# Two self-attention layers in fp32: hand-ordered queues, two more split steps, and projections moved between layers

## The chip, the cores and the metric

The kernel runs on one core of a Trainium2 chip. Five engines work side by side, each with its own queue of instructions: TensorE (PE, matrix products; PEld is its weight load), VectorE (DVE), ScalarE (ACT), GpSimd (POOL, which here only issues DMAs) and SyncE (SP, which issues DMAs as well). The metric is the time of one execution on the device in microseconds (us); the kernel before takes 3156.2 us, the median of three runs (3154.14 to 3157.11).

## The reference

The input x is 4 images of 64x64 = 4096 tokens with 256 channels. Each layer is attention of all tokens of an image with each other. Layer 0 has queries and keys of 32 channels and values of 256, and a residual with a factor gamma; layer 1 has values of 128 channels and an output matrix to 256.

```python
# layer 0
q = x @ Wq + bq; k = x @ Wk + bk; v = x @ Wv + bv
attn = softmax(q k^T)
x = gamma * (attn @ v) + x
# layer 1
f = x @ Wf + bf; g = x @ Wg + bg; v = x @ Wh + bh
beta = softmax(g f^T)
out = x + (beta @ v) @ Wo + bo
```

All of it is fp32. The matrix of 4096x4096 scores of each image and layer is never stored; it is made and used up tile by tile.

## The kernel before, in words

**fp32 from cheaper products.** [...] So the kernel can split a factor p into `high`, `low` and a difference `d`, the values likewise into three forms, and add three fp32r products (a *split* step), or it takes one true fp32 product (a *whole* step). Splitting costs a second exponential on ACT (L542, `high`) beside the first (L544, `p`), and two passes on DVE (L555 `low`, L560 `d`). In layer 0 every step is split. In layer 1 the steps named in SPLIT1 are, 6 of 16.

**Steps and blocks.** Work is a list of steps, in the order image b, layer l, query block j, step i. In layer 0 a block has 256 queries and eight steps of 512 keys; there are 16 blocks, 128 steps an image. In layer 1 a block has 512 queries and 16 steps of 256 keys; there are 8 blocks, again 128 steps. Each step has an exponential of 128x1024 elements. Iteration n of the main loop (L738) issues the `d` of step n (`cut_both`), the `low` of step n+1 (`cut_low`), the sum of p (`add_up`, layer 1 only, L573), the scores and exponentials of step n+2 (`later.scores`, L532), units of other work, and the products of step n (L582 in layer 0, L600 in layer 1).

**Sums.** In layer 0 the sum of the exponentials comes out of the products (two more columns in the values). In layer 1 DVE adds p into `p_sum` (L571, L573); for the five steps in MOVED_SUMS a DMA that accumulates does it (L548, L550, issued by POOL), and its result is added at the block's end (L662), followed by the fold of two halves (L663).

**Projections.** Tokens go in halves of 256, 16 an image. For each half and layer there are three units: `transpose_unit` (eight DMAs load 32x32 squares, L280; DVE transposes, L392; ACT and DVE cut the result into `xh` and `xl`, L405, L406), `qk_unit` (four matmuls L422, then ACT and DVE in turn, L439 to L442, and a store to `qk_dram`, from where POOL loads keys and queries, L493), and `v_unit` (matmuls L464 and the cut of the values, L480 to L487). Layer 1's halves need the result of layer 0's blocks, which goes through `x1_dram` (L636).

**Where they stand.** `plan` puts units into iterations. In layer 0, block j projects half j-2 for layer 1; the last two halves come in layer 1's first block. The next image's halves, queries, keys and values alike, are projected in layer 1, one every seven steps. `ends` finish a block in the next one's first iterations: residuals in layer 0 (L629 to L643), outputs in layer 1 (L670 to L678).

**What sets the order.** The program is traced in this order, but the framework's planner then orders each engine's instructions anew, by priority and by its own estimate of when they are ready, before the kernel is built. On the chip each engine's queue is fixed.

**Buffers.** The 128x1024 tiles live in named rings: two of `t`, three of `p`, two of `l`, one of `d` and one of `e`, nine in all (L267). The squares, `xh` and `xl` share a ring of two. PSUM holds the accumulators, `st` for scores, `pair` (accumulators in layer 0, a second scores buffer in layer 1) and two side buffers.

Of the kernel before, what the change touches and what calls it, by code (L numbers as in the profile page):

```python
# [65 lines left out]
AHEAD = 3  # L66

SPLIT1 = (0, 3, 5, 8, 11, 13)
MOVED_SUMS = (0, 4, 7, 9, 12)
# [169 lines left out]
def fast_path(ctx: ExitStack, tc: tile.TileContext, x, w0, w1, wo, bo, gamma, out, off):  # L239
# [15 lines left out]
    V1 = NI[1] - sum(split[1])  # L255

# [8 lines left out]


    def wide(tag, name, dtype=F32):  # L267
        return work.tile([P, 2 * QB], dtype, tag=tag, bufs={"d": 1, "e": 1, "p": 3}.get(tag, 2), name=name)

# [36 lines left out]
    ident = const.tile([P, P], F32, name="ident")  # L306
# [12 lines left out]
    bv = const.tile([P, C], F32, name="bv0")  # L319
# [3 lines left out]
    bo_sb = const.tile([P, C], F32, name="bo")  # L323
    for l, (q_w, q_b, k_w, k_b, v_w, v_b) in enumerate((w0, w1)):
        queue = (nc.scalar, nc.gpsimd)[l]
        w_sb = work.tile([P, NCC, 2 * D], F32, tag="small", bufs=4, name=f"wqk_whole{l}")
        b_sb = const.tile([2 * D, 1], F32, name=f"bqk{l}")
        for g, w_dram, b_dram in ((0, q_w, q_b), (D, k_w, k_b)):
            queue.dma_start(w_sb[:, :, g : g + D], w_dram.rearrange("(c p) d -> p c d", p=P))
            queue.dma_start(b_sb[g : g + D, :], b_dram.rearrange("(d o) -> d o", o=1))  # L330
# [9 lines left out]
    nc.gpsimd.dma_start(bv, w0[5].partition_broadcast(P))  # L340
    nc.gpsimd.dma_start(bv1, w1[5].rearrange("(c o) -> c o", o=1))
    nc.gpsimd.dma_start(wo_sb, wo)
    nc.gpsimd.dma_start(bo_sb, bo.partition_broadcast(P))
# [16 lines left out]
    def bias_units():  # L360


        def issue():
            nc.vector.tensor_scalar(bv, bv, gamma_sb, None, ALU.mult)
            wide_bias = work.tile([P, P], F32, tag="small", bufs=4, name="wide_bias")
            nc.vector.memset(wide_bias, 1.0)
            nc.vector.tensor_scalar(wide_bias, wide_bias, bv1, None, ALU.mult)
            ps = side_psum("ps_bias")[:, :C]
            nc.tensor.matmul(ps, wide_bias, wo_sb, start=True, stop=True)
            nc.vector.tensor_add(bo_sb, bo_sb, ps)  # L370

        return [issue]

    xT, x_parts, k_t, v_t, halves = {}, {}, {}, {}, {}
    qk_dram, x1_dram = {}, {}
    q_t, moved_sums, first_p, waiting = {}, {}, [], {}


    def transpose_unit(b, l, h):
        def issue():  # L380
            key = (b, l, h)
            lead = b == l == 0 and h % 2 == 1
# [8 lines left out]
            else:  # L391
                nc.vector.transpose(  # L392
                    xT[key].rearrange("p c n -> p (c n)"), turned[key].rearrange("p c n -> p (c n)")
                )
            x_parts[key] = [
# [9 lines left out]
            nc.scalar.copy(x_parts[key][0], xT[key])  # L405
            nc.vector.tensor_sub(x_parts[key][1], xT[key], x_parts[key][0].bitcast(F32))  # L406
# [3 lines left out]
        return issue  # L410

    def project_units(b, l, h):

        key = (b, l, h)
        j, part = divmod(h, 2)
        cols = slice(part * QB0, (part + 1) * QB0)

        def qk_unit():
            ps = side_psum(f"psqk_{b}_{l}_{h}")[:, :QB0]
            for c in range(NCC):  # L420
                for n in range(2):
                    nc.tensor.matmul(  # L422
                        ps,
                        wqk[l][:, c, :],
                        x_parts[key][n][:, c, :],
                        start=(c == n == 0),
                        stop=(c == NCC - 1 and n == 1),
                    )
            whole = data.tile([2 * D, QB0], F32, tag="qk", name=f"qk_{b}_{l}_{h}")
            lead = b == l == 0 and h % 2 == 1  # L430
            parts = data.tile(
# [6 lines left out]
            top, bottom = slice(0, 2 * D), slice(2 * D, P)  # L438
            nc.scalar.copy(whole, ps[bottom, :])  # L439
            nc.vector.scalar_tensor_tensor(whole, ps[top, :], bqk[l], whole, ALU.add, ALU.add)  # L440
            nc.scalar.copy(parts[top, :], whole)
            nc.vector.tensor_sub(parts[bottom, :], whole, parts[top, :].bitcast(F32))  # L442

            if part == 0:
                qk_dram[b, l, j] = dram.tile([2, 2, D, QB], F32, name=f"qk_dram_{b}_{l}_{j}")
            nc.sync.dma_start(qk_dram[b, l, j].rearrange("h w d n -> (h w d) n")[:, cols], parts.bitcast(F32))
            halves[b, l, j] = part + 1
            if l == 0 and b > 0:
                load_half(b, h + 1)
            elif l == 1 and h == NH - 1:  # L450
                load_half(b + 1, 0)
            elif l == 1:
                load_squares((b, 1, h + 1), waiting.pop((b, h + 1)))
# [6 lines left out]
        def v_unit():  # L460
            ps = side_psum(f"psv_{b}_{l}_{h}")[:, : NS * CV[l]].rearrange("p (t c) -> p t c", c=CV[l])
            for t in range(NS):
                for c in range(NCC):
                    nc.tensor.matmul(  # L464
                        ps[:, t, :],
                        xT[key][:, c, t * P : (t + 1) * P],
# [3 lines left out]
                    )  # L470
            seen = seen_v[:, l, b * NH + h : b * NH + h + 1]
            if split[l][h if l == 1 else 0]:
                if l == 0:
                    tiles = slice(part * NS, (part + 1) * NS)
                    high, low, d = (v0[j][what][:, tiles, :C] for what in ("h", "l", "d"))
                else:
                    t = data.tile([P, 3 * NS, P], F32R, tag="v1_parts", bufs=sum(split[1]), name=f"v_{b}_{h}")
                    high, low, d = (t[:, n * NS : (n + 1) * NS, :] for n in range(3))
                    v_t[b, h] = {"h": high, "l": low, "d": d}
                nc.scalar.activation(high, ps, AF.Copy, scale=1.0 - DOWN)  # L480
                nc.scalar.activation(low, ps, AF.Abs, accum_out=seen)
                nc.vector.scalar_tensor_tensor(d, high.bitcast(F32), -1.0 - EPS, ps, ALU.mult, ALU.add)
                nc.vector.scalar_tensor_tensor(low, d.bitcast(F32), UP, high.bitcast(F32), ALU.mult, ALU.add)
# [5 lines left out]
        return [transpose_unit(b, l, h), qk_unit, v_unit]  # L489
# [19 lines left out]

    def small(name):  # L510
        return work.tile([P, C], F32, tag="small", bufs=4, name=name)


    class Step:


        def __init__(self, b, l, j, i):
            self.b, self.l, self.j, self.i = b, l, j, i
            self.first, self.last = i == 0, i == NI[l] - 1
            self.split = split[l][i]  # L520
            self.key = f"{b}_{l}_{j}_{i}"

        def scores(self):
# [15 lines left out]
            s_flat = st.rearrange("p g n -> p (g n)")  # L539
            if self.split:  # L540
                self.high = wide("t", f"high_{self.key}", F32R)
                nc.scalar.activation(self.high, s_flat, AF.Exp, bias=down)  # L542
            self.p = wide("t" if self.split and l == 1 else "p", f"p_{self.key}")
            nc.scalar.activation(self.p, s_flat, AF.Exp)  # L544
            if l == 1 and i in MOVED_SUMS:
                if i == MOVED_SUMS[0]:
                    moved_sums[b, j] = wide("e", f"p_sum_moved_{b}_{j}")
# [4 lines left out]
        def cut_low(self):  # L552
            if self.split:
                self.low = wide("l", f"low_{self.key}", F32R)
                nc.vector.tensor_sub(self.low, self.p, self.high.bitcast(F32))  # L555

        def cut_both(self):
            if self.split:
                self.d = wide("d" if self.l == 0 else "l", f"d_{self.key}", F32R)
# [4 lines left out]
        def add_up(self, p_sum):  # L564
            if self.l == 0 or self.i in MOVED_SUMS:
                return
            kept = [i for i in range(NI[1]) if i not in MOVED_SUMS]
            if self.i == kept[0]:
                first_p.append(self.p)
            elif self.i == kept[1]:  # L570
                nc.vector.tensor_add(p_sum, first_p.pop(0), self.p)  # L571
            else:
                nc.vector.tensor_add(p_sum, p_sum, self.p)  # L573

        def products_first(self, acc, s, what):
# [5 lines left out]
            for g in range(G[0]):  # L581
                nc.tensor.matmul(  # L582
                    acc[2 * s + which][:, :width],
                    p[:, g * QB0 + s * P : g * QB0 + (s + 1) * P],
# [5 lines left out]
        def products_second(self, acc, parts):  # L590
            v = v_t[self.b, self.i]
            for part in parts:
# [6 lines left out]
                for g in range(G[1]):  # L599
# [3 lines left out]
                        p[:, g * QB : (g + 1) * QB],  # L603
# [3 lines left out]

# [5 lines left out]
    def end_first(b, j, acc):  # L613
# [265 lines left out]
```

## Time and profile before

| | before |
|---|---|
| median of three runs | 3156.2 us |
| profiled execution | 3153.35 us |
| its span, first to last instruction | 3151.5 us |
| granted TensorE clock, mean | 0.998 |
| PE busy | 3118.5 us, 99% |
| DVE busy | 2597.9 us, 82% |
| ACT busy | 2140.4 us, 68% |
| mean busy share of the DMA engines, layer 0 and layer 1 of the third image | 0.32 and 0.59 |

A row of a group reads: line, engine, operation, out<-in with shapes, count, busy us, mean ns of one, then the idle time before it and what ended it. In the view in order of time, a row is start, length, engine, line, operation and count; the idle time before it stands in brackets. A matmul's end is modelled, so its rate is read from the starts of successive ones.

### The profile page before, as it was taken

How to read it: one execution, taken by the hardware profiler on the slowest of the kernel's cores; microseconds unless marked ns; L12 is line 12 of the kernel's file. 1: busy time of each engine (PE TensorE's matmuls, PEld its weight loads, DVE VectorE, ACT ScalarE, POOL GpSimd, SP SyncE). 2: the span in 40 equal slices, each digit the busy share in tenths (PEclk: the TensorE clock that was granted, in tenths of full speed). 3: DMA queues.
4: the chain of work that ended last, by engine and by line, in shares of the span. 5: the costliest groups of instructions: out<-in, count | busy, mean ns of one | idle time of the engine just before them, and what ended most of it. 6: DMA issues, size and time to landing. Idle time of an engine off the chain costs nothing.

```text
span 3151.5 us, 54031 instructions
## 1 busy us (share of the span) xinstructions
PE 3118.5 (99%) x19908; PEld 2674.6 (85%) x19908; DVE 2597.9 (82%) x3237; ACT 2140.4 (68%) x2835; POOL 745.9 (24%) x1108
## 2 busy tenths in 40 slices
PE   8999999999999999999999999999999999999998
PEld 7999998666799999866679999976668999997665
DVE  7788888888888888888888888888987888888886
ACT  7666666777666666777766666677776666666665
POOL 5111113222311111322241111132223111123222
PEclk9999999999999999999999999999999999999999
DMA  6732325555532232555543222365565223235544
GB/s 181 204 63 56 58 55 109 107 110 101 107 58 56 53 63 55 114 105 109 107 96 60 56 56 56 59 120 108 102 113 94 52 52 63 56 72 108 95 94 82
DMA packets 428255, 273.06 MB, mean 87 GB/s; under 512 B 270768, under 2 KB 392112, under 8 KB 427984
## 3 DMA queue, kind: packets, MB, share of 16 engines
q0 software_dynamic: 105024, 168.43, 29.8%
q1 hardware_dynamic: 322048, 100.76, 13.6%
q8 instruction: 161, 2.64, 0.4%
q14 instruction: 110, 0.90, 0.1%
q10 hardware_dynamic: 912, 0.33, 0.0%
HBM read 82.58 MB, written 83.89 MB: 53 GB/s over the span
## 4 chain that ended last, share of the span: by engine, by line
PE 90%; DVE 3%; issue 1%; DMA 1%; ACT 1%; SPq 0%; DVEq 0%; ACTq 0%; POOLq 0%
PE acc L600 23%; PE acc L582 23%; PE acc_pair L582 23%; PE st L532 14%; PE psv L464 4%; PE pso L670 2%; PE psqk L422 2%; DVE low L555 1%; DVE p_sum L573 1%; ACT p L544 1%; DVE d L560 1%; PE pso L671 0%; DMA p_sum_moved<-p 0%; DMA squares<-in_x 0%; DMA squares<-x_dram 0%
## 5 line engine op out<-in xcount | busy, mean ns | idle before, releaser
L542 ACT ACTIVATE high<-st,down 128x1024 fp32r<-128x1024 f32 x704 | 786.4, 1117 | 704.0 <-DVE low L555 321.5
L544 ACT ACTIVATE p<-st 128x1024 f32<-128x1024 f32 x1024 | 1042.9, 1022 | 170.5 <-PE st L532 148.8
L560 DVE SCALAR_TENSOR_TENSOR d<-low,high 128x1024 fp32r<-128x1024 f32 x704 | 859.9, 1221 | 316.8 <-PE acc_pair L582 311.2
L555 DVE TENSOR_TENSOR low<-p,high 128x1024 fp32r<-128x1024 f32 x704 | 859.7, 1221 | 146.7 <-ACT p L544 145.7
L532 PE MATMUL st<-q,k 128*128 128x256 f32 (+1 forms) x3072 | 706.7, 339 | 4.7 <-DMA k<-qk_parts 2.4
L600 PE MATMUL acc<-p,v 128*128 128x512 f32 x1280 | 611.1, 597 | 0.0
L532 PEld LDWEIGHTS st<-q,k 128*128 128x128 f32 x3072 | 470.6, 189 | 105.4 <-issue 40.3
L600 PEld LDWEIGHTS acc<-p,v 128*128 128x128 f32 x1280 | 233.4, 190 | 161.6 <-issue 143.3
L573 DVE TENSOR_TENSOR p_sum<-p_sum,p 128x1024 f32<-128x1024 f32 x288 | 350.7, 1218 | 9.4 <-ACT p L544 5.8
L582 PE MATMUL acc<-v0h,high 128*128 128x258 f32 x2048 | 342.3, 284 | 1.2 <-ACT high L542 1.2
L582 PE MATMUL acc<-v0d,d 128*128 128x258 f32 x2048 | 339.3, 287 | 1.7 <-DVE d L560 1.6
L643 POOL DMA_DIRECT2D out<-x x128 | 112.8, 883 | 943.4 <-DVE x L632 896.3
L582 PE MATMUL acc_pair<-v0h,high 128*128 128x258 f32 x2048 | 330.5, 283 | 0.0
L582 PE MATMUL acc<-v0l,low 128*128 128x256 f32 (+1 forms) x2048 | 329.9, 283 | 0.2
L582 PE MATMUL acc_pair<-v0d,d 128*128 128x258 f32 x2048 | 329.0, 283 | 0.0
L582 PE MATMUL acc_pair<-v0l,low 128*128 128x256 f32 (+1 forms) x2048 | 328.8, 282 | 0.0
L582 PEld LDWEIGHTS acc<-v0h,high 128*128 128x128 f32 x2048 | 286.5, 189 | 3.1 <-issue 1.4
L582 PEld LDWEIGHTS acc<-v0d,d 128*128 128x128 f32 x2048 | 281.9, 190 | 4.3 <-DVE d L560 3.7
L582 PEld LDWEIGHTS acc<-v0l,low 128*128 128x128 f32 x2048 | 282.7, 190 | 1.1 <-DVE low L555 0.6
L582 PEld LDWEIGHTS acc_pair<-v0h,high 128*128 128x128 f32 x2048 | 282.7, 190 | 0.0
L582 PEld LDWEIGHTS acc_pair<-v0l,low 128*128 128x128 f32 x2048 | 281.6, 190 | 0.0
L582 PEld LDWEIGHTS acc_pair<-v0d,d 128*128 128x128 f32 x2048 | 281.6, 190 | 0.0
(108 smaller groups left out, 3288.7 us busy)
## 6 DMA issues: line engine op xcount, KB each, us to landing
p_sum_moved<-p POOLq DMA_DIRECT2D x160, 512.0 KB, 4.8
x_res<-in_x SPq DMA_DIRECT2D x128, 128.0 KB, 2.3
qk_dram<-qk_parts SPq DMA_DIRECT2D x128, 128.0 KB, 1.9
x_res<-bv POOLq DMA_DIRECT2D x128, 128.0 KB, 3.3
out<-bo SPq DMA_DIRECT2D x128, 128.0 KB, 2.5
x_dram<-x SPq DMA_DIRECT2D x128, 128.0 KB, 1.7
out<-x POOLq DMA_DIRECT2D x128, 128.0 KB, 3.2
squares<-x_dram SPq DMA_DIRECT2D x512, 32.0 KB, 1.9
```

The lines of the kernel that those rows point to most:

```text
L422: nc.tensor.matmul(ps, wqk[l][:, c, :], x_parts[key][n][:, c, :], start=(c == n == 0), stop=(c == NCC - 1 and n == 1),)
L464: nc.tensor.matmul(ps[:, t, :], xT[key][:, c, t * P : (t + 1) * P], wv[l][:, c, :], start=(c == 0), stop=(c == NCC - 1),)
L532: nc.tensor.matmul(st[:, g, :], k_t[b, l, kt // NT][:, kt % NT * P : (kt % NT + 1) * P], q_t[b, l, j * n // QB][:, q0 : q0 + n], start=Tru ...
L542: nc.scalar.activation(self.high, s_flat, AF.Exp, bias=down)
L544: nc.scalar.activation(self.p, s_flat, AF.Exp)
L555: nc.vector.tensor_sub(self.low, self.p, self.high.bitcast(F32))
L560: nc.vector.scalar_tensor_tensor(self.d, self.low.bitcast(F32), -UP, self.high.bitcast(F32), ALU.mult, ALU.add)
L573: nc.vector.tensor_add(p_sum, p_sum, self.p)
L582: nc.tensor.matmul(acc[2 * s + which][:, :width], p[:, g * QB0 + s * P : g * QB0 + (s + 1) * P], v0[self.i][v][:, g, :width], start=self.f ...
L600: nc.tensor.matmul(acc[which], v_part[:, g, :], p[:, g * QB : (g + 1) * QB], start=first and g == 0, stop=last and g == G[1] - 1,)
L643: nc.gpsimd.dma_start(out_rows(b, j, s), x_new[s], accum_op=ALU.add)
L670: nc.tensor.matmul(ps[:, :C], part, wo_sb, start=True, stop=True)
```

## The change

- **Split steps.** SPLIT1 becomes the eight even steps. Six sums instead of five are moved to DMA (five in the very last block), on other steps, and the DMA is issued one stage later (`move_sum`).
- **Order.** From the ninth step on, `tc.manual_schedule()` switches the planner off: every engine's queue is the order of the program text. Units are cut into stages (matmul, take on ACT, add on DVE, cut, rest), and each is put on a step and a place: "a" ahead of the step's `d`, "b" after its scores. DVE's sums go into a list `later_sums` and are issued when two counters (`tensor_clock`, `vector_clock`) say that DVE has room, or after at most three steps.
- **Projections.** In layer 0, block j projects half j-1 for layer 1 and the queries and keys of half j-1 of the next image. The transposed tokens are stored to DRAM (`xT_dram`) and loaded again in layer 1, where only the values of the next image are projected.
- **Buffers.** The wide tiles come from eight equal buffers; the one that is expected to be free first is taken. In layer 1 the values' tiles of layer 0 that aren't in use yet serve as further ones. The bias rows live in DRAM and not in SBUF.
- **Ends.** ACT takes layer 0's accumulators in the last step already; the outputs of layer 1 stand at steps 9, 10, 12 and 13 of the next block, and the moved sums are added from its second step on. The checks over all sums are done during the last blocks, but for the last eight columns.

```diff
-SPLIT1 = (0, 3, 5, 8, 11, 13)
-MOVED_SUMS = (0, 4, 7, 9, 12)
+OUT_AT = (9, 10, 12, 13)
+MOVED_AT = 1
+KEEP, AHEAD_OF = 3, 1.0
+Q_AHEAD = 6
+VALUES_AT = [(0, ())] + [(2 * j - 2, (3, 7)) for j in range(1, 6)] + [(10, (1, 5, 9)), (13, (1, 5, 9))]
+WIDE = 8
+MANUAL_FROM = 8
+SPLIT1 = (0, 2, 4, 6, 8, 10, 12, 14)
+MOVED_LAST = (3, 5, 7, 9, 11)
+MOVED_SUMS = (3, 5, 7, 9, 11, 14)
...
+    def wide(name, until, dtype=F32):
...
+        which = min((k for k in free_at if may_have(k)), key=free_at.get)
+        free_at[which] = until
+        while any(held is not None and held == in_slot.get(which) for _, _, _, held in later_sums):
+            later_sums.pop(0)[2]()
...
+        if not isinstance(which, int):
+            return v0[which[0]][which[1]][:, :, :C]
+        return work.tile([P, NT, QB0], dtype, tag=f"wide{which}", bufs=1, name=name)
...
         def add_up(self, p_sum):
...
+            later_sums.append((1.15, self.n + (KEEP if self.n < last_block else 1), issue, f"p_{self.key}"))
...
+        n_next += j < NQ[0] - 1
+        put(n_next, "b", residual(0))
+        put(n_next + 1, "b", residual(1))
...
+    def put_half(n, b, h, at):
+        (turn, cut, rest), qk, v = project_stages(b, 1, h)
+        load = lambda: load_squares((b, 1, h), x1_rows(b, h))
+        put_all(n, at, (load, turn, cut, rest, qk[0], qk[1], qk[2], qk[3], qk[4], v[0], v[1], v[2]))
+
+    def put_next(n, b, h, at):
+        (turn, cut, rest), qk, v = project_stages(b, 0, h)
+        def keep():
+            turn()
+            xT_dram[b, h] = dram.tile([P, NCC, QB0], F32, name=f"xT_dram_{b}_{h}")
+            nc.sync.dma_start(xT_dram[b, h], xT[b, 0, h])
+        load = lambda: load_half(b, h)
+        put_all(n, at, (load, keep, cut, rest, qk[0], qk[1], qk[2], qk[3], qk[4]))
...
+    def plan(n, b, l, j):
+        if l == 0 and j >= 1:
+            put_half(n, b, j - 1, "3b 5b 5b 6b 7b 8a 8b 8b 9b 8b 9a 11b")
+            if b + 1 < B:
+                put_next(n, b + 1, j - 1, "0b 1b 1b 2b 3b 4a 4b 4b 5b")
+        if l == 1:
+            if j == 0:
+                put_half(n, b, NH - 1, "2b 5a 5b 6a 7b 8a 8b 8b 9a 8b 9a 9b")
+            if b + 1 < B:
+                if j == 0:
+                    put_next(n, b + 1, NH - 1, "9b 11a 11b 12a 13b 14a 14b 14b 15b")
+                else:
+                    first, at = VALUES_AT[j]
+                    for k, m in enumerate(at):
+                        put_values(n + m, b + 1, first + k)
...
+        if n == MANUAL_FROM:
+            ordered.enter_context(tc.manual_schedule())
...
+        run(todo.pop((n, "a"), []))
+        s.move_sum()
+        if l == 0:
+            s.cut_both()
+            after.cut_low()
+        else:
+            cost = 1.9 if s.split else 2.2
+            tensor_clock += cost + 1.7 * (b + 1 < B and s.i in (3, 7)) + 0.63 * (j > 0 and s.i in OUT_AT)
+            vector_clock = max(vector_clock, tensor_clock - cost)
+            s.cut_both()
+            after.cut_low()
+            vector_clock += 1.15 * (s.split + after.split)
+            s.add_up(p_sum)
```

## The prediction

> **What bounds the kernel now.** I read the page's busy shares first.
>
> ```profile
> PE 3118.5 (99%) x19908; PEld 2674.6 (85%) x19908; DVE 2597.9 (82%) x3237; ACT 2140.4 (68%) x2835; POOL 745.9 (24%) x1108
> ```
>
> TensorE (PE) is never seen idle for long, with VectorE (DVE) next at 82%. A busy PE need not be at its full rate, so I took the two layers of the third image apart (busy time by stretch; the boundaries are where the scores L532 change from four 256-column matmuls to two of 512).
>
> ```profile
> 1620.00:2074.00 454.00, 453.60 (x3763) 451.24 (x3762) 368.25 (x455) 298.17 (x378) 88.20 (x127) 1.00 0.32 60
> 2074.00:2396.00 322.00, 321.31 (x1202) 214.41 (x1202) 281.91 (x343) 234.19 (x329) 92.54 (x139) 1.00 0.59 114
> ```
>
> Columns: PE, PEld, DVE, ACT, POOL busy, the granted clock (1.00) and the DMA share. DVE is 368.25 of 454 (81%) in the first layer, 281.91 of 322 (88%) in the second. Next, the pace of PE in order of time.
>
> ```profile
> 302.96 0.64 PE L582 MATMUL acc<-v0h,high 128*128 128x258 f32 x4
> ...
> 306.31 0.65 PE L582 MATMUL acc<-v0h,high 128*128 128x258 f32 x4
> ```
>
> One first-layer step is 3.35 us for 28 matmuls: 0.12 us each, with no gap between groups. Eight steps plus one half's projections (keys and queries 0.47, values 0.89) make 28.2; sixteen make 451 of the 454. So PE is at its own rate.
>
> ```profile
> 3114.12 0.62 PE L600 MATMUL acc<-high,v 128*128 128x512 f32 x2
> 3114.58 0.62 PE L600 MATMUL acc<-low,v 128*128 128x512 f32 x2
> 3115.03 0.62 PE L532 MATMUL st<-q,k 128*128 128x512 f32 x2
> 3115.49 1.88 PE L600 MATMUL acc<-p,v 128*128 128x512 f32 x4
> 3116.80 1.03 PE L600 MATMUL acc<-d,v 128*128 128x512 f32 x2
> 3117.66 0.63 PE L532 MATMUL st<-q,k 128*128 128x512 f32 x2
> ```
>
> In the second layer a split step's `high` and `low` products take 3115.03 - 3114.12 = 0.91 us for four matmuls, 0.228 each, and its two `d` products 0.455: 1.365 in all. From 3115.49 to 3117.66 lie one whole step and one `d`: 2.17 - 0.455 = 1.715 for the whole step. Scores are 0.455. A block of 16 steps (ten whole, six split, four outputs of 0.65) is 7.28 + 17.15 + 8.19 + 2.6 = 35.2 us; eight of them less the first one's outputs, sixteen halves of the next image (0.47 + 1.73) and two of its own (1.36) give 317 of the measured 322. All that a better order could win in steady state is thus 3 + 5 us an image, and some of it is only rounding of the pace.
>
> **The change, part by part.**
>
> **Two more split steps.** Per block two whole steps become split: 1.715 - 1.365 = 0.35 us each, 8 blocks x 4 images x 2 = 64 times: **-22.4 us**. The Trainium skill ("TensorE: Matmul & The Clock Gate", section "Back-to-back issue gap") gives N/2.4 + 2.5 ns, 215.8 for 512 columns, so six products 1.295; with four passes of 0.427 for a true FP32 product ("FP8 and Floating Point Precision", "TensorE Precision Notes") a whole step is 1.71 and the gain 0.41 x 64 = 26.6. The trace has 228 ns, so I take 22.4. What a split adds lies on other engines: ACT one L542 (1.117), DVE an L555 and an L560 (2 x 1.221). One more sum in each block is moved to a DMA (six instead of five), which takes an L573 (1.218) off DVE.
>
> **DVE in the second layer**, by durations: 16 x 1.221 + 9 sums x 1.218 + the moved sum 1.221, fold 0.69, `o` 0.83, reciprocals 0.66 = 33.9 us a block, with two value halves (2 x 1.37) 36.6. PE: 7.28 + 8 x 1.715 + 8 x 1.365 + 2.6 = 34.5, with two halves 38.0. It fits, closely. What hides DVE is PE's 1.4 us; without that cover each block costs what it is over. The exception is the first block of each layer: 25 wide operations (30.5), a half of its own (2.28), one of the next image (2.28), two residuals (1.58), a value cut (0.83) = 37.5 against PE's 34.6. Sums may be put off into the next block (two of them, 2.4 us), so between 0 and 2.9; I take 0.5.
>
> **Queries and keys of the next image in the first layer.** On PE 0.47 us a half moves from one layer to the other: 0 in the sum. Every half brings along its eight loads (L280), the transpose 0.706, the cut on ACT, L406 0.685, L440 0.471, L442 0.419, one store (L446), and new: a store of xT and a later reload for the values. The first-layer block becomes, on PE, 28.2 + 0.47 = 28.7; on DVE 16 x 1.221 + two halves' 2.28 + half a value cut 0.42 + ends 2.43 = 26.9 (94%). The mean fits; one stretch is tight. In step 1 DVE has 1.92 us of extra work (L442, a transpose, a residual), in step 2 1.48. The steady order is: `low` ends 2.56 us into step 1, extra work, then `d`, which PE needs 2.39 us into step 2, at 5.74: room 5.74 - 2.56 - 1.22 = 1.96 for 1.92. Over both steps (a 0.47 projection gives PE time) the room is 3.35 for 3.40. Does an operation cost its duration?
>
> ```profile
> 300.08 1.22 DVE L560 SCALAR_TENSOR_TENSOR d<-low,high 128x1024 fp32r<-128x1024 f32 x1
> 301.25 1.23 DVE L555 TENSOR_TENSOR low<-p,high 128x1024 fp32r<-128x1024 f32 x1
> 302.39 0.48 DVE L632 SCALAR_TENSOR_TENSOR x<-o,g,x_res 128x256 f32<-128x256 f32 x1
> 303.16 1.23 DVE L560 SCALAR_TENSOR_TENSOR d<-low,high 128x1024 fp32r<-128x1024 f32 x1 [0.29 <-PE acc_pair L582]
> ```
>
> Back to back, starts are 1.17 and 1.14 apart, 0.06 under the duration. The skill ("VectorE: DVE Perf Modes", section on the TRN2 errata) has (N+151)/0.96 = 1.224 us for 1024 fp32 elements: by this rule, which speaks against the change, PE waits 0.05 us a block plus every semaphore; by the trace's spacing about 0.3 us is spare. The 0.29 in the last row is a wait for the single `d` buffer, which goes with the pool of eight. I take 0.1 us for each of 45 blocks (15 x 3 images): **+4.5**; range 0 to 22.
>
> **The loads.** The half of block j-1 is now loaded in block j itself, not a block later.
>
> ```profile
> SPq L280 <- DMA x_dram<-x: 40.7, 42, 2.6
> ```
>
> ```profile
> L280 SPq DMA_DIRECT2D squares<-x_dram x512: 303/449/1896, 105.5 to 2863.7; - x171
> ```
>
> (First SP's waits: us, times, longest; then the row of the tile `squares`: ns shortest/median/longest.) Eight issues of 0.449 are 3.6 us. The second residual ends 1.3 us into step 3, its store lands 1.7 later, the loads are issued by 6.6 and land 1.9 later, at 8.5: 1.3 us into step 5 (steps 3 and 4 are 3.83 + 3.35). The transpose is reached at about 2.6. So the load is hidden with 1.3 us to spare, and DVE, a strict queue, can lose about 1 us more before PE sees it: cost 0.
>
> **Hand-ordered queues.** In layer 2 the third image's 322 against 317 is what the present order loses; I give back 4 us in each of three images: **-12** (0 to -20). New waits, since now nothing is pulled ahead: at the start of each second layer the third step's scores need `pair`, which DVE empties first (two L620, about 0.9 us with the semaphore); there the last half's chain residual, store, loads, transpose, projection, store, key loads must end before step 12. Step by step I find its transpose up to 2 us late on DVE, of which PE sees 0.3, and the keys 0 to 3 us late (POOL issues four at 0.577 behind a moved sum), take 1. With the 0.5 above 2.7 x 4 = **+11**. In blocks 7 and 8 an output waits for a side buffer that DVE frees late: 0.5 x 6 = **+3**. The moved sums now follow each other every two steps (3.9 us) but take 4.8 us to land: they run up to 3.6 us late, covered by p buffers held longer.
>
> **Start and end.** The first eight steps keep the planner's order; the bias now goes over DRAM: 0 to +3, take +1. At the end the checks over all sums are done earlier.
>
> ```profile
> 3142.01 0.29 DVE L814 TENSOR_SCALAR good<-inverse 128x256 f32<-128x256 f32 x1 [1.81 <-DMA out<-y]
> ...
> 3144.89 0.15 DVE L828 CAST off<-count 1x1 int32<-1x1 f32 x1 [0.37 <-PE count L827]
> ```
>
> The 1.81 us for a buffer goes, and some 1.4 of the chain; the last output's landing (issued until 3142.4, 3.2 us) hides part: **-2**.
>
> Sum: -22.4 + 4.5 - 12 + 11 + 3 + 1 - 2 = -17 us. The profiled execution took 3153.35 (span 3151.5), the runs' median is 3156.2; 17 off that is **3139**, and I forecast 3138, -0.6%.
>
> **Rivals.** *No new waits:* only -22.4 - 12 - 2, and a little of the start's 28 us: about 3118. For it: DVE spacing leaves room everywhere but one block in eight. Against: strict queues.
> *The second layer's DVE takes it all back:* each block there at the 36.6 us of DVE plus the waits for PE at its ends; 0.6 us in 32 blocks returns 19 us: 3156. For it: 88% DVE already, and the change adds 64 x 2.44 - 31 x 1.22 = 118 us of DVE work there, less 36 an image moved away.
> *Slower, the first layer waits for its loads:* the transpose of the half meets its loads late (sixteen loads a block now, and the slowest landing in the trace is 6.8 us), DVE stands, and `d` comes late. From 0.5 us a block the 22 us are gone; at 1 us x 45 blocks it is 3138 + 45 = 3183. Against it: 1.3 us of margin, DMA only a third busy in this layer.
> *The split doesn't shorten a step* can't be, as both kinds are in the trace.
>
> **How the numbers follow.** A measurement here can tell 0.2%, 6 us. The forecast (3121 to 3149) 0.58; no new waits 0.14; taken back (3150 to 3162) 0.11; slower 0.17. Faster 0.72, same 0.11, slower 0.17. The likeliest case's own range is 3121 to 3149; from 3114 to 3170 leaves out some two in ten.
>
> **What would show it.** Right: whole products x1024, `d`, `high`, `low` x512 each, PE records 20036; second layer about 309 us, first about 461 in images 0 to 2 and 454 in the last; blocks of the last image 34.5. Wrong, if DVE's idle time before L392 or L406 grows by tens of us, if PE idles before L532 or `d` in the first layer, or if PE's pace differs with operands in another layout.

## The result

The changed kernel takes 3156.4 us (median; 3152.7 to 3161.2) against 3156.2 beside it: a ratio of 1.0002, 95% interval 0.9993 to 1.0011. Nothing changed that can be measured; the forecast was 3138. Its profiled execution has a span of 3155.9, 4.4 us more than before. The busy shares of its page, and the two layers of its third image by stretch (columns as in the prediction):

```profile
PE 3099.8 (98%) x20036; PEld 2696.1 (85%) x20036; DVE 2755.2 (87%) x3360; ACT 2203.1 (70%) x2899; POOL 773.2 (24%) x1137
```

```profile
1618.00:2077.00 459.00, 457.02 (x3804) 455.06 (x3805) 406.98 (x515) 319.95 (x424) 91.75 (x133) 1.00 0.46 92
2077.00:2397.50 320.50, 313.81 (x1191) 216.84 (x1189) 281.41 (x310) 227.62 (x298) 97.50 (x145) 0.99 0.60 121
```

PE is busy for 18.7 us less, and the span grew all the same. The first layer has 459 us (forecast 461, before 454) with DVE at 89% and PE hardly ever stopped. The second has 320.5 where 309 was forecast, and PE is busy for only 313.8 of it. Layer by layer, from the first exponential `p` of one layer to that of the next (the last layer of image 3 to the end of the span):

| us | image 0 | 1 | 2 | 3 |
|---|---|---|---|---|
| layer 0 before | 496.6 | 454.7 | 453.9 | 454.0 |
| layer 0 after | 497.9 | 458.6 | 459.4 | 451.2 |
| layer 1 before | 322.7 | 322.0 | 321.9 | 301.6 |
| layer 1 after | 317.5 | 319.1 | 320.4 | 306.9 |
| of it, first block before | 37.2 | 37.2 | 37.2 | 34.7 |
| of it, first block after | 43.7 | 44.7 | 43.3 | 38.9 |

This mark is late in one place: in the kernel before, ACT does other work between `high` and the first `p` of a second layer (in image 1 they start at 1295.58 and 1298.02 us). Counted from the layer's first scores on PE, the first blocks had 38.5, 38.5, 38.5 and 36.8 us and have 43.7, 44.8, 43.4 and 38.9, and the four first layers grew by 12.9 us in all, not by the 7.9 of the table.

The steady second-layer block became shorter (40.1 to 38.5 us, in the last image 35.5 to 35.0; in the first three images some 0.9 of it is matmuls that moved to the first layer). The **first block** of each second layer became longer, by 5.2, 6.3, 4.9 and 2.1 us from the first scores, with nearly the same matmul work in it (36 us at the paces of the prediction). PE's stops in it add up to 4.6, 5.8, 4.4 and 2.3 us; before, to 0.2, 0.2, 0.2 and 0.5. Here it is in image 1 of the changed kernel, in order of time: the rows before which PE was idle, then those before which DVE waited for a transfer, then SP's issues.

```profile
1303.21 0.72 PE L595 MATMUL st<-q,k 128*128 128x512 f32 x2 [0.59 <-DVE o L693]
1321.07 1.22 PE L673 MATMUL acc<-v0l,v 128*128 128x512 f32 x2 [3.55 <-DVE v0l L625]
1336.14 0.71 PE L595 MATMUL st<-q,k 128*128 128x512 f32 x2 [0.71 <-DMA k<-qk_dram]
1338.27 0.73 PE L673 MATMUL acc<-v0d,v 128*128 128x512 f32 x2 [0.96 <-DVE v0d L625]
```

```profile
1319.19 0.71 DVE L403 STREAM_TRANSPOSE xT<-squares 128x512 f32<-128x512 f32 x1 [2.84 <-DMA squares<-x_dram]
1336.40 0.71 DVE L403 STREAM_TRANSPOSE xT<-squares 128x512 f32<-128x512 f32 x1 [2.87 <-DMA squares<-in_x]
```

```profile
1305.75 0.33 SPq L708 DMA_DIRECT2D x_dram<-x  x1
1307.74 0.32 SPq L469 DMA_DIRECT2D qk_dram<-qk_parts  x1
1308.65 0.32 SPq L708 DMA_DIRECT2D x_dram<-x  x1
1310.63 4.38 SPq L287 DMA_DIRECT2D squares<-x_dram  x8
1329.89 0.34 SPq L469 DMA_DIRECT2D qk_dram<-qk_parts  x1
1330.33 3.85 SPq L287 DMA_DIRECT2D squares<-in_x  x8
```

Read from below. The second residual's store is issued at 1308.65; the eight loads of squares that need it run until 1315.0 in SP's queue and land near 1319. The last of them takes 4.31 us from issue to landing, the longest of all loads of squares (median 1.9); two moved sums of 512 KB are under way in that stretch, and whether they hold it up was not tried. DVE meets the transpose 2.84 us too early and stands, with the `low` of a later step queued behind it; PE stands 3.55 us for that `low` (it bears the name of the buffer, `v0l`). SP's next entry, the store of the projected keys, waits until 1329.89 for DVE, and the next image's eight loads stand behind it, though the input has been there all along. PE waits 0.71 us for the keys, which come out of that store; DVE stops a second time, at 1336.40, and PE 0.96 us for the `low` behind it. The long stop for the half's own squares is image 1's alone: in the other three images it is the keys that PE stands for, 1.1 to 3.0 us.

### The profile page after: what moved, and what is told of

The parts are those of the page before. It is cut to its first block, busy times and chain, and to the rows that moved or that the text cites. A ratio compares the mean times of both kernels' runs of the same rounds, so it can differ in the third digit from the quotient of the medians.

```text
span 3155.9 us, 55119 instructions
## 1 busy us (share of the span) xinstructions
PE 3099.8 (98%) x20036; PEld 2696.1 (85%) x20036; DVE 2755.2 (87%) x3360; ACT 2203.1 (70%) x2899; POOL 773.2 (24%) x1137
## 5 line engine op out<-in xcount | busy, mean ns | idle before, releaser
L605 ACT ACTIVATE high<-st,down 128x1024 fp32r<-128x1024 f32 x645 | 721.0, 1118 | 696.1 <-PE st L595 605.2
L611 ACT ACTIVATE p<-st 128x1024 f32<-128x1024 f32 x1024 | 1026.5, 1019 | 17.2 <-DMA p_sum_moved<-p 9.7
L625 DVE TENSOR_TENSOR low<-p,high 128x1024 fp32r<-128x1024 f32 x534 | 652.7, 1222 | 123.8 <-ACT p L611 119.4
L595 PE MATMUL st<-q,k 128*128 128x256 f32 (+1 forms) x3072 | 663.4, 324 | 13.3 <-DMA k<-qk_dram 7.4
L630 DVE SCALAR_TENSOR_TENSOR d<-low,high 128x1024 fp32r<-128x1024 f32 x527 | 643.0, 1220 | 15.6 <-PE acc L673 0.7
L673 PE MATMUL acc<-p,v 128*128 128x512 f32 x1024 | 488.8, 600 | 1.1 <-DVE o L744 1.1
L655 PE MATMUL acc<-v0h,high 128*128 128x258 f32 x2048 | 330.9, 284 | 1.2 <-ACT high L605 1.2
L644 DVE TENSOR_TENSOR p_sum<-p_sum,p 128x1024 f32<-128x1024 f32 x257 | 313.0, 1218 | 0.3
L673 PEld LDWEIGHTS acc<-p,v 128*128 128x128 f32 x1024 | 188.4, 191 | 144.2 <-issue 123.6
L655 PEld LDWEIGHTS acc_pair<-v0d,d 128*128 128x128 f32 x2048 | 281.6, 189 | 0.0
```

The costliest lines, as they stand in the source:

```text
L595: nc.tensor.matmul(st[:, g, :], k_t[b, l, kt // NT][:, kt % NT * P : (kt % NT + 1) * P], q_t[b, l, j * n // QB][:, q0 : q0 + n], start=Tru ...
L630: nc.vector.scalar_tensor_tensor(self.d, self.low.bitcast(F32), -UP, self.high.bitcast(F32), ALU.mult, ALU.add)
L644: nc.vector.tensor_add(p_sum, other, self.p)
L655: nc.tensor.matmul(acc[2 * s + which][:, :width], p[:, g, s * P : (s + 1) * P], v0[self.i][v][:, g, :width], start=self.first and what != ...
L673: nc.tensor.matmul(acc[which], v_part[:, g, :], p[:, g * NS : (g + 1) * NS, :], start=first and g == 0, stop=last and g == G[1] - 1,)
```

## The experiments

Two theories. **A**: in the fixed queues transfers at the start of each second layer are waited for, and that ate the gain. **B**: DVE takes the two extra split steps back (the second rival of the prediction).

| kernel | split steps | ratio to before, 95% | first blocks of layer 1, us | steady block |
|---|---|---|---|---|
| after, repeated | 8 | 1.0005 (0.9997 to 1.0013) | 44.9 / 45.4 / 42.6 / 39.5 | 38.5 |
| split6 | 6 | 1.0022 (1.0015 to 1.0029) | 42.8 / 42.5 / 39.8 / 37.0 | 39.1 |
| early | 8 | 0.9998 (0.9989 to 1.0007) | 42.9 / 43.2 / 41.2 / 41.8 | 38.5 |
| next_late | 8 | 1.0007 (0.9999 to 1.0016) | 42.8 / 40.6 / 40.4 / 42.6 | 38.5 |
| chain | 8 | 0.9975 (0.9963 to 0.9986) | 43.2 / 38.8 / 39.1 / 38.4 | 38.5 |
| packed, first time | 8 | 0.9976 (0.9969 to 0.9982) | 38.3 / 38.3 / 38.6 / 38.4 | 38.5 |
| packed, repeated | 8 | 0.9968 (0.9955 to 0.9980) | 41.3 / 38.5 / 38.7 / 38.3 | 38.5 |
| packed | 6 | 0.9986 (0.9979 to 0.9992) | 36.9 / 37.0 / 36.6 / 36.6 | 39.1 |

### One part of the change at a time

**Six split steps**, the rest of the change kept (label split6):

```diff
-SPLIT1 = (0, 2, 4, 6, 8, 10, 12, 14)
+SPLIT1 = (0, 3, 5, 8, 11, 13)
```

> The changed kernel with six split steps again (0, 3, 5, 8, 11, 13), everything else as changed. Theory A (the two more split steps do gain 64 x 0.35 = 22 us on TensorE, and the gain is lost elsewhere: in the first block of each second layer and at the end): the waits of the first blocks stay and the 22 us are missing, so about 3156 + 20 = 3172 to 3178 us. Rival B (VectorE bounds the whole second layer, so that the splits gain nothing): with less VectorE work the time stays at 3150 to 3158.

Measured 3162.7, ratio 1.0022. Between the two: the extra splits are worth 6 us in all, though the steady blocks differ by 0.6 us in each of some thirty. (The moved sums and all else keep the places chosen for eight splits; places of their own for six were not tried.) Where they stand is the last comparison below.

**The planner's order** for the new program (label planner): `MANUAL_FROM` beyond the last step.

> The changed kernel with the planner's order on all steps, the program text otherwise the same. Theory A (VectorE stands at a transpose whose loads have not landed, because the queue is fixed in the text's order): the planner moves other work ahead of it, TensorE's idle time in the four first blocks falls from about 30 us to under 10, and the time is 3125 to 3145. Rival C (the work as it now lies, not its order, costs the time): within 5 us of 3156. Rival D (the planner's estimates are worse for this split of work): over 3165.

Measured 3323.8, 1.0531. Most of that is the start: the first five blocks of the very first layer take 333 us and not 183, with PE waiting for `d` and `low` (41 us at once), and DVE before them for transfers (63 and 42 us before transposes). Past it the same program loses less: its first layers have 458.6, 458.6 and 450.4 us in images 1 to 3, no more than in the hand order, and its second layers 322.8, 323.6, 323.1 and 311.1, 16.7 more in all. So past the start the hand order gains in the second layers alone.

**The extra splits alone**, in the kernel before (label bsplit8); to fit, the bias rows go to DRAM, and the identity and the keys' intermediate share other tiles:

```diff
-SPLIT1 = (0, 3, 5, 8, 11, 13)
-MOVED_SUMS = (0, 4, 7, 9, 12)
+SPLIT1 = (0, 2, 4, 6, 8, 10, 12, 14)
+MOVED_SUMS = (3, 5, 7, 9, 11, 14)
```

> The kernel before with the eight even steps split and six moved sums, in the planner's order, with projections and all else where they were; only the bias rows and the temporary of queries and keys lie where the change puts them, to make room. Theory A (a split step is 0.35 us shorter on TensorE, and VectorE has room when the order is free): 3156 - 22 and up to 8 us of new VectorE waits, 3134 to 3142. Rival B (VectorE bounds the second layer): 3150 or more.

Measured 3557.9, 1.1271. That is not the splits alone. In the first image's first layer, where the pattern of splits is as before, 666 us stand against 497: by the releasers that the profile names, DVE waits there 74 us for squares and 61.5 at once for a transfer of the bias rows (`out<-bias`). This points to the edits that made room, or to the order that the planner found for them, and not to the pattern. The second layers have 367 to 375 us and not 302 to 323, 221 more in all, and there PE stops for exponentials and for `d`. First two waits of the kernel before, then four of this one (us in all, times, longest; L532 and L536 are the scores, L604 the second layer's products):

```profile
DVE d L560 <- PE acc_pair L582: 311.2, 347, 1.5
PE st L532 <- ACT p L544: 1.4, 5, 0.6
```

```profile
DVE d L564 <- PE acc_pair L586: 295.3, 327, 2.2
PE st L536 <- ACT p L548: 59.7, 81, 2.5
PE acc L604 <- DVE d L564: 44.4, 44, 1.5
PE acc L604 <- ACT high L546: 25.1, 43, 1.6
```

The longest wait, DVE's for the one buffer of `d`, stood in the kernel before as well and cost nothing there; it explains nothing here. As built, with nine tiles in fixed rings, the bias rows in DRAM and the planner's order, the pattern loses; which of these does it was not separated.

**Most of the moved projections undone** (label back11): eleven of sixteen halves of the next image get queries and keys in the second layer again.

```diff
-            if b + 1 < B:
+            if b + 1 < B and j >= 11:
                 put_next(n, b + 1, j - 1, "0b 1b 1b 2b 3b 4a 4b 4b 5b")
...
+                if j < 5:
+                    put_next(n, b + 1, 2 * j, "7b 10a 10a 10b 11a 11b 11b 11b 12a" if j else "8b 10a 10a 10b 11a 11b 11b 11b 12a")
+                    put_next(n, b + 1, 2 * j + 1, "11b 14a 14a 14b 15a 15b 15b 15b 15b")
```

> Undoes most of the move: eleven of the sixteen halves of the next image (0 to 9 and 15) get their queries and keys in the second layer again, two a block in its blocks 0 to 4. PE's work only changes place. By my sum DVE has 36.6 us in such a block and gets 4.6 more, against 39.4 of PE: about 1.8 us over in four blocks and 4 in the first, 11 x 3 images, less what the first layer's waits were (0.1 to 0.5 a block): about 3185. If DVE is not what bounds the second layer: 3156.

Measured 3225.0, 1.0222; worse than expected. A block with two such halves has 43.6 to 44.7 us (38.5), the first layer only 5 us less in images 1 and 2. In 1390 to 1434 us:

```profile
1390.00:1434.00 44.00, 40.75 (x155) 27.65 (x155) 38.83 (x46) 31.16 (x43) 11.18 (x16) 1.00 0.69 139
```

DVE has 38.8 us of work and 4.9 of waits in it, all for ACT, 3.8 of them in the stages of the projection; PE stops for DVE and ACT in turn. What a strict queue costs is thus its work *and* the waits of what is put into it. This placing was mine; a better one may cost less. That the second layer has no room for these halves next to eight splits is what it shows.

### The start of the second layer

**The half's squares loaded early** (label early; for the last half they are read from another half's rows, so that the load needn't wait):

```diff
-                put_half(n, b, NH - 1, "2b 5a 5b 6a 7b 8a 8b 8b 9a 8b 9a 9b")
+                put_half(n, b, NH - 1, "0b 5a 5b 6a 7b 8a 8b 8b 9a 8b 9a 9b")
```

> The changed kernel, but the last half of each second layer is loaded two steps earlier and from the half before last of the same image, which has long been stored; so the queries, keys and values of that half are those of other tokens, and the work is otherwise the same. Theory A (the chain residual, store, eight loads, transpose stops VectorE in the first block, and TensorE with it): the idle time of VectorE before the transpose of x1's squares goes, the second stop (at the next image's squares, loaded behind it) goes with it, and the time falls by 20 to 30 us, to 3126 to 3136. Rival C (the first block has too much VectorE work): no more than 8 us less, 3148 or more.

Measured 3155.3, 0.9998: no gain. The stop is gone and another has taken its place (same block, PE; DVE waits 4.2 us for the next image's squares):

```profile
1317.58 0.73 PE L673 MATMUL acc<-v0l,v 128*128 128x512 f32 x2 [0.60 <-DVE v0l L625]
1333.07 1.19 PE L595 MATMUL st<-q,k 128*128 128x512 f32 x2 [2.67 <-DMA k<-qk_dram]
```

The keys of the last half are needed at a fixed step. As long as their stages stand on the same steps, an earlier load only changes which entry of the chain is waited for.

**The next image's last half later** (label next_late): its stages at `9b 14a 14b 15a 16b 17a 17b 17b 18b`.

> The next image's last half five steps later, nothing else. Theory W: DVE's wait of 2.9 to 4.4 us for the next half goes, but PE's stops for the half's squares and the keys stay: first blocks of images 0 to 2 about 42.5, the last image unchanged, 3151. Theory D: 3156.

Measured 3155.3, 1.0007. DVE's second stop goes, PE still waits 2.4 us for the keys.

**The whole chain packed** (label chain): both residuals in one step, the load a step earlier, the keys stored in step 8 and not 9.

```diff
-        put(n_next + 1, "b", residual(1))
+        put(n_next + (j < NQ[0] - 1), "b", residual(1))
...
-                put_half(n, b, NH - 1, "2b 5a 5b 6a 7b 8a 8b 8b 9a 8b 9a 9b")
+                put_half(n, b, NH - 1, "1a 5b 6a 6b 7a 7b 7b 8a 8a 8b 9a 9b")
```

> As the run before, without the later half of the next image and without the change at the end. Theory W: the wait for the half's squares (2.8 to 2.9 us) and most of that for the keys (0.7 to 3.0) go, the one for the next half (2.9 to 4.4) stays on DVE: first blocks about 41, 3147. Theory D: 3153 or above.

Measured 3145.2, 0.9975. **Packed and later**, with the order at the very end changed too (labels chain_late_tail, and packed_same beside the changed kernel):

> Both residuals of the last first-layer block in one step, the last half's stages packed one to two steps closer (keys stored in step 8 and not 9), the next image's last half five steps later, and at the very end the o sums ahead of the moved sum. Theory W (the 6 to 9 us by which each second layer's first block is over its products are three transfers that DVE or PE stands for: the half's squares, the next half's squares, the keys): first blocks fall from 43.3 to 44.7 to about 39 and in the last image from 38.9 to 37, so 5 x 3 + 2 = 17 us less and 1.4 at the end: about 3138. Theory D (DVE has 37.5 us of work in that block, and the transfers only hide it): first blocks stay at 42 or more, 3150 or above.

> The changed kernel once more, so that it stands beside the next three on one chip: 1.000 of before, first second-layer blocks 43 to 45 us.

> The kernel with the packed stages once more. If the waits at the start of the second layers are worth what the first look said, it is 8 us or more below the run before it, in one and the same count, 0.9976 of before. If that was the chip, 0.999 or above.

Measured 3143.7 (0.9976) the first time; the second time 3145.7 (0.9968) where the changed kernel has 3157.6 (1.0005). That is 12 us between the two on one chip, and faster than the kernel before as well. In the repeated run's trace the block of image 1 looks like this (PE):

```profile
1303.89 0.73 PE L595 MATMUL st<-q,k 128*128 128x512 f32 x2 [0.58 <-DVE o L693]
1319.08 0.39 PE L439 MATMUL psqk<-xh,wqk 128*128 128x256 f32 x1 [0.53 <-ACT xh L418]
1320.14 0.38 PE L439 MATMUL psqk<-xl,wqk 128*128 128x256 f32 x1 [0.67 <-DVE xl L421]
```

The waits for squares and keys are gone; 1.2 us for the packed stages are new (`xh` and `xl` both come after the transpose in DVE's queue). The four first blocks have 156.8 us in the repeated run against 172.4 in the changed kernel beside it, 15.6 less (image 0's varies from run to run: 38.3, 41.3, and 43.2 in the run with the chain alone); the second blocks get 2.6 of work that was moved there. So theory A holds for 12 us. The run with the next half later alone (no gain), the load early alone (no gain) and the chain packed alone (all of it) show which link it was: the one from residual to keys. The changed order at the end added nothing that can be told apart.

**Two attempts to go on** fell short. With the projection half a step later, other places for the values and the moved sum of the last block earlier (label less_waiting, and with six splits):

```diff
+                put_half(n, b, NH - 1, "1a 5b 6a 6b 7b 8a 8b 8b 8b 8b 9a 9b")
...
+    put(len(steps) - 1, "b", lambda: nc.vector.tensor_add(p_sum, p_sum, moved_sums[B - 1, NQ[1] - 1]))
```

> Goes on from the run with the packed stages: the projection of the last half half a step later (PE stands 1.2 us there for its two halves, in each of four images), value halves of blocks 7 and 8 at steps 1, 4 and 7 and not 1, 5 and 9 (an output waits 1.9 us for a side buffer in the third image, less in the others), and the moved sum of the very last block added one step earlier (PE stands 2.1 us before the last outputs and then has a clock of 0.50 for eight groups of matmuls, 1.5 us more). If each stop is a loss of its own: 5 + 3 + 3 us less than 3143.7, so 3133 by the same count, 0.994 of before. If DVE bounds these places anyway the stops come back a few steps later: 3143.

> The same with six split steps in the second layer (0, 3, 5, 8, 11, 13), the change's other parts kept. The steady blocks of after and of its variant with six splits differ by 0.6 us (38.45 and 39.1; last image 35.05 and 35.6). If the waits around the first block were what ate the gain of the splits, the whole of it appears here: 32 blocks x 0.6 = 19 us slower than the run before (PE alone by my forecast: 22). If DVE takes it back wherever the waits are gone, the two differ by 6 as with the first order (3162.7 against 3156.4).

Measured 3150.8 (0.9984) and 3152.6 (0.9992). The keys are stored that half step later, and PE waits 0.5 to 0.8 us for them again; the middle first blocks grew to 42, and PE stands 2.9 us for an exponential where the last image begins. And with the next image's last half moved into the first layer's first block (label dve_relieved, then relieved_same beside the packed kernel):

```diff
+        if l == j == 0 and 0 < b < B - 1:
+            put_next(n, b + 1, NH - 1, "0b 1b 1b 2b 3b 4a 4b 4b 5b")
```

> The packed stages (first such run: 3143.7 us, 0.9976 of before) with DVE relieved where its queue is full: the next image's last half, 2.3 us of DVE work in the second layer's first two blocks, goes into the first block of the first layer for images 1 and 2 (which has no projection; DVE 24 of 29 us there), and at the very end the moved sum is added before the last p sum, the fold after the o sums. If DVE's queue is what still costs there: first blocks 38.3 to 37.5, second ones 40.2 to 38.5 (PE's 0.5 us gone with them), so 2.5 x 2, less 0.5 x 2 in the first layer, and 2 at the end: 6 us, 0.9957 of before. If only transfers counted, PE's half us changes place and nothing is won: 0.9976.

> The same with six split steps (0, 3, 5, 8, 11, 13). In the run before with six (3152.6) against eight (3150.8) 19 us of shorter steady blocks had shrunk to 2. If a full DVE queue at the layer's edges is where they went, relief must let more of them through: 8 us or more between these two. If they are lost elsewhere, 2 to 6 as before.

> The kernel with the next image's last half in the first layer once more. In its trace the second blocks had shortened as expected (40.2 to 39.3), and the first blocks of the first layer had grown by 2.2 us in two images. If these two are all, it is within 3 us of the packed kernel; if moving that half is a loss, 6 or more slower.

Measured 0.9994, and 0.9984 beside the packed kernel's 0.9968, 4.7 us slower; with six splits 1.0004. The second blocks shortened as expected (40.2 to 39.2), but the first layer's first blocks stop longer in exchange: PE stands 2.1 us there for a side buffer that ACT frees late.

### What the extra splits are worth once the waits are gone

The packed kernel with six split steps (label packed_six):

> The packed kernel with six split steps. If VectorE takes the extra splits back wherever they stand, it is 2 to 6 us slower than the run before it. If the waits had eaten them, 15 or more slower. Its first second-layer blocks should be 37.5 or less (eight splits: 38.3), the steady ones 39.1 (38.5).

Measured 3151.3 (0.9986) against 3145.7 (0.9968): 5.7 us. One first block and one steady block, by stretch: six splits, then eight.

```profile
1300.20:1337.20 37.00, 36.42 (x150) 24.45 (x149) 30.37 (x36) 26.41 (x36) 9.92 (x15) 1.00 0.58 116
1377.00:1416.00 39.00, 39.00 (x142) 25.78 (x141) 30.01 (x33) 26.40 (x35) 10.37 (x15) 1.00 0.58 115
```

```profile
1299.50:1338.00 38.50, 36.72 (x156) 25.60 (x155) 35.13 (x43) 27.99 (x39) 9.91 (x15) 1.00 0.59 119
1378.00:1416.50 38.50, 38.50 (x146) 26.56 (x145) 34.24 (x37) 28.05 (x37) 10.56 (x15) 1.00 0.60 115
```

In the steady block eight splits win 0.6 us, with DVE at 34.2 of 38.5 and PE never stopping. In the first block they lose 1.5: DVE has 35.1 of 38.5, PE 1.8 us of stops. Over the four images the first blocks give back 9.7 us (156.8 against 147.1; some 3 of it is image 0's, whose first block varies from run to run), the second blocks of three images 1.8 (40.2 against 39.6), and two single places about 2.6. So theory B holds too, not in the steady blocks, where the rival looked for it, but at each layer's edges.

## Why the prediction was wrong

The profiled span should have fallen by 17 us and rose by 4.4. Counted from first scores to first scores, and with the forecast's terms put where they belong (21.2 us of moved matmuls change layers): the start and the first layers grew by 13.6 us (forecast 26.7), the first blocks of the second layers by 18.5 (8.2), and their other blocks with the end shrank by 27.8 (51.8). By the steps of the sum:

- **Two more split steps, -22.4.** The mechanism is right, the term a little too large: a block with two more of them is 0.6 us shorter in the same order (39.1 to 38.5), 0.3 a step and not 0.35 (0.41 was the estimate from the pages' figures). That is 19 for all 64 if nothing else gave way.
- **The start of each second layer, +11 in "Hand-ordered queues".** This step failed. The first blocks are 18.5 us longer in all, and that with two splits more in each, which should have shortened them by 0.6: some 21 and not 11. I had counted the chain (residual, store, loads, transpose, projection, store, keys) as "up to 2 us late on DVE, of which PE sees 0.3", and the keys as 1 us late. In the trace DVE stood 2.8 us and PE 3.6 in image 1, and PE 1.1 to 3.0 for the keys in the other images; in three of the four the clock fell as well. What was left out or too small: the eight loads need 4.4 us of SP's queue after the store has landed (3.6 in my count for the first layer) and the last one 4.3 to land (1.9); a stop of DVE passes to PE whole when `low` stands right behind it; and the next image's loads stand behind a store that itself waits for DVE. Packing the chain takes 12 us off the median, so this much is shown.
- **DVE in the first block, 0.5 of it.** I had the right sum (37.5 us of work against 34.6 of PE) and took 0.5 of "between 0 and 2.9", since sums can be put off. With the waits gone eight splits still cost 1.7 us more there than six, in steady blocks 0.6 less: 2.3 a block, near the upper end of my range.
- **Hand-ordered queues, -12.** This failed as well. I gave back 4 us an image as what the old order loses, and it lost nothing that an order can win: in the seven later blocks of image 1 PE's stops add up to 0.2 us in the kernel before and 1.1 in the changed one. These blocks have 284.7 us for 281.6 of matmuls at the paces of the prediction before, and 274.4 for 269.2 now. The 3 to 5 us were rounding of the pace, as I had noted and then not used. Only beside the planner's order of the new program is the hand order worth something, 16.7 us in the second layers.
- **The first layer, +4.5 and +1 at the start.** Too dark. A steady block grew by 0.4 us (28.2 to 28.6), where 0.47 of matmuls moved in and 0.1 of waits was put on top; 21 us moved in, and the four layers grew by 12.9. The loads that the third rival feared are hidden and DVE kept up: PE stops 1.2 to 1.9 us in each of the last three first layers, most of it at their very start. This error went the other way and hid some 13 us of the miss, which is luck.
- **Blocks 7 and 8, +3.** About right in kind: in the third image an output waits 1.9 us for its side buffer, in the others less.
- **The end, -2.** It became about +3: the last block and the end have 56.0 us and not 53.8, with 0.6 less to do. DVE adds the moved sum and folds before the last `o`, so PE stands 2.33 us and not 0.90; then the last outputs run at half the clock. From the last cast to the span's end pass 10.5 us and not 6.6; a part of it appears with the hand order whatever else is in the kernel (below).

The time came out at the second rival's 3156, by other sums than its own: the price of the splits was paid in other blocks than it named, and half of the miss is a chain of transfers that no rival had.

## What to carry to other kernels

When a planner is switched off, walk each dependent chain (store, load, engine, store, load) through *every* queue it touches and write down what stands behind each entry; a late entry costs what the one behind it is due for. A chain with a fixed due step must be shortened as a whole: freeing one link only shows the next. And a sum of work per steady block says nothing of a layer's first block: here DVE was near 90% in the steady state, and the edges decided whether the saving on PE was kept. Last, before time is given back to a better order, look for the stops that it would end: a gap between a block and the sum of its matmuls need not be one.

## What the runs showed of the hardware

**What a split buys.** In the rows of the prediction a whole step's two fp32 products leave four matmul records and take 1.715 us; two products of one split form, in the type fp32r, leave two records and take 0.455. Three forms make 1.365.

**A short stop costs clock.** After PE's 3.55 us stop in the first block, this stretch of the changed kernel (granted clock in the third column from the right):

```profile
1321.20:1325.50 4.30, 4.30 (x13) 3.02 (x13) 4.20 (x5) 2.67 (x4) 0.86 (x1) 0.63 0.49 91
```

4.3 us at 0.63 is, by estimate, 1.6 us of matmuls lost on top; read finer, the clock is 0.50 up to 1324.3 and 1.00 from 1324.5 on. At the end 2.33 us were enough:

```profile
3139.06 0.70 PE L754 MATMUL pso<-wo,o 128*128 128x256 f32 x2 [2.33 <-DVE o L744]
3140.64 1.22 PE L754 MATMUL pso<-wo,o 128*128 128x256 f32 x2
```

The same pair takes 0.70 and, 1.6 us later, 1.22. The Trainium skill ("TensorE: Matmul & The Clock Gate", Part 1, on the HAM clock gate) has the clock at half rate after an idle window of some 3.4 us that runs freely; the first case agrees, the second came after less. In the packed kernel's first run two stops of 0.58 and 1.49 us with two matmuls between them did it too, with a clock of 0.50 from 3126 to 3130 us. The 0.90 us stop of before did not. Nor does the length alone decide: in the run with the next half later, 2.40 us of stop (up to 1333.10) are followed by 1.00, while 1.94 us in the changed kernel (up to 2384.90) are followed by 0.50 from 2386.0 to 2389.3. What share of a window has to be idle no run here shows.

**The end of the program.** From the last cast (L981) to the span's end pass 10.5 us in the changed kernel, 9.9 to 11.1 in the other fourteen runs in hand order, 7.6 in the planner's order of the same program, 8.3 in the kernel before with eight splits, 6.6 before. The difference lies in a drain of POOL's queue, 4.56 us in each of the fifteen and 2.64, 2.72 and 2.02 in the other three, and in the branch ahead of it. In the changed kernel the last output has landed some 3 us before that drain begins. What makes it longer stays open.
